# A two-layer non-local block: key products in other banks, theta and transposes at other places, reciprocals a batch sooner

## The chip, the cores and the metric

The kernel runs on one core of one Trainium2 chip. The metric is the device time of one execution in microseconds. Before the change five runs gave 2532.21 to 2532.64 us, with a median of 2532.59 us. One more execution was recorded by the hardware profiler. The engines are named as the profile names them: PE multiplies matrices, PEld loads its weights, DVE is the vector engine, ACT the scalar engine, SP issues DMAs (SPq is its queue).

## The reference

Two layers of the same block are applied to `x` of shape (4, 128, 96, 96) in float32. One layer computes, with `CI` = 64:

```python
g_x     = maxpool2(conv1x1(x, g_w, g_b)).reshape(b, CI, -1).transpose(0, 2, 1)   # values, 2304 keys
theta_x = conv1x1(x, theta_w, theta_b).reshape(b, CI, -1).transpose(0, 2, 1)      # 9216 queries
phi_x   = maxpool2(conv1x1(x, phi_w, phi_b)).reshape(b, CI, -1)                   # keys
f    = einsum('bqc,bck->bqk', theta_x, phi_x)
attn = softmax(f, axis=-1)
y    = einsum('bqk,bkc->bqc', attn, g_x).transpose(0, 2, 1).reshape(b, CI, H, W)
W_y  = conv1x1(y, W_w, W_b)
inv  = bn_gamma * rsqrt(bn_var + 1e-5)
return W_y * inv + (bn_beta - bn_mean * inv) + x
```

## The kernel before, in words

The work is eight blocks (four images by two layers, in the order `ORDER`). A block has nine pairs of query tiles; a pair is 1024 queries (`PT`, two tiles of `QT` = 512). The 2304 keys of a block are 18 tiles of 128 (`NKT`), and two key tiles make a batch (`KB`), so that a pair takes nine batches (`NB`).

The main loop runs over `t`, one batch of one pair for each `t`. In a batch PE makes the scores of two key tiles (`scores`, four products for each tile), ACT takes the exponential of each tile (128x1024, `exp`), DVE adds it to a running sum (`add_up`), and PE multiplies the exponentials of the batch before by the transposed values `gT` (`values`, result `av`). Two pairs make a cycle of 18 batches (`CYCLE`). In it `q` is the number of the cycle's first pair and `s` the batch within the cycle. All else is laid into the cycle at fixed places: the products for new keys (`chunks`) and for new queries (`thetas`) in two halves, one in a batch and one in the next; denominators, reciprocals and the projection with `W` of the pairs that have ended. The order on every engine is that of the code; nothing is rescheduled.

PSUM is cut into three pools: `ps_sc` with two tiles of two banks (scores), `ps_av` with one tile of two banks, and `ps_misc` with two tiles of one bank. Each pool hands out its tiles in turn, so a new tile waits for the readers of the one before the last.

Ahead of the loop the first twelve key tiles of block 0 are made (`FIRST` = 6 batches). A key tile is one group of two products with all 128 input rows (`pooled`, result `gphi_ps`, one bank) and one DVE reduction over 2x2 pixels (`pool`, L226). `batch` then has ACT subtract the mean of the first two key tiles (`centred`, L270) and copy the result to the other half of the partitions (`copied`, L276). In the same stretch come the transposes of the weights (`make_gphi`, `make_theta`, `first_cols`), two square roots with a change of ACT's table, and at its end the queries of the first pair (`theta`, `take_theta`). `square(i, k)` has DVE transpose the values of six key tiles into `gT`, two instructions for each `k`; four of the twelve quarter transposes of block 0 stand ahead of the loop, and the others stand in the loop at the batches that `squares` lists.

In the last cycle (`q == late`) the reciprocals of the pair before the last (`inverses`) stand one in each of four batches, then `normalise` and, at `t == total - 1`, `multiply` and `add`. `ends` holds some `values` products back to that point. The last pair's own denominators follow (`last_denominators`, L374 and L382), then the held products, and the output (`finish`).

Of the kernel before, what the change touches and what calls it, by code (L numbers as in the profile page):

```python
# [9 lines left out]
F32 = mybir.dt.float32  # L10
# [6 lines left out]
P = 128  # L17
B, C, CI, H, W = 4, 128, 64, 96, 96
HW = H * W
NK = (H // 2) * (W // 2)  # L20
QT = 512
# [11 lines left out]
PT = 2 * QT  # L33
NP = HW // PT
KB = 2
# [3 lines left out]
THETAS, SUMS, PROJECT = 5, 2, (8, 12)  # L39
# [9 lines left out]
def shifted_blocks(ctx: ExitStack, tc: tile.TileContext, x: bass.AP, layers, out: bass.AP, flag):  # L49
# [27 lines left out]
    ps_sc = ctx.enter_context(tc.tile_pool(name="ps_sc", bufs=2, space=PSUM))  # L77
    ps_av = ctx.enter_context(tc.tile_pool(name="ps_av", bufs=1, space=PSUM))
    ps_misc = ctx.enter_context(tc.tile_pool(name="ps_misc", bufs=2, space=PSUM))
# [28 lines left out]
    def transposed(src, rows, cols, name, twice=False, ps=None):  # L108
        if ps is None:
            ps = ps_misc.tile([P, QT], F32, tag="misc", name=f"{name}_ps")  # L110
        nc.tensor.transpose(ps[:cols, :rows], src, ident[:rows, :rows])
        t = const.tile([2 * cols if twice else cols, rows], F32, name=name)
        nc.vector.tensor_copy(t[:cols, :], ps[:cols, :rows])
        if twice:
            nc.vector.tensor_copy(t[cols:, :], ps[:cols, :rows])
        return t

    class Layer:
# [22 lines left out]
        def make_gphi(self):  # L141
            self.gphi = transposed(self.gphi_nat, 2 * CI, C, f"gphiT_{self.l}")

        def make_theta(self):
            self.theta = transposed(self.theta_nat, CI, C, f"thetaT_{self.l}")

        def make_scale(self):

# [41 lines left out]
    def two_banks(name):  # L190
        return [ps_misc.tile([P, QT], F32, tag="misc", name=f"{name}_{i}") for i in range(2)]
# [12 lines left out]
    class Block:  # L204
# [25 lines left out]
                ALU.max,  # L230
            )

        def pooled(self, k):

            ps = ps_misc.tile([P, QT], F32, tag="misc", name=f"gphi_ps_{self.name}_{k}")
            for c in range(2):
                nc.tensor.matmul(
                    ps[ts(c, CI), :], lhsT=self.w.gphi[:, ts(c, CI)],
                    rhs=self.chunk(k, slice(0, P)), start=True, stop=True,
                )  # L240
            self.pool(k, ps)

        def chunks(self, j):

# [233 lines left out]
    def denominators(both, folded):  # L478

        pss = two_banks(f"den_ps_{both[0].name}")  # L480

        def make():
            for h in range(2):
                for i in range(len(both)):
                    nc.tensor.matmul(  # L485
                        pss[i][ts(h, CI), :], lhsT=ones[ts(i, CI), :],
                        rhs=folded[ts(i, CI), ts(h, QT)], start=True, stop=True,
                    )

        def take():  # L490
            for pair, ps in zip(both, pss):
                pair.take_denominators(ps, pair.halves[:, QT:])

        return make, take

    def thetas(both):
        pss = two_banks(f"theta_ps_{both[0].name}")

        def part(i, rows, c):
            pair = both[i]  # L500
            return (
                pss[i][ts(c, CI), :], pair.blk.w.theta[rows, :],
                pair.blk.xt[rows, ts(2 * pair.p + c, QT)],
            )

        def take():
            for i in range(2):
                both[i].take_theta(pss[i])

        return crosswise(part, take)  # L510

    ws = [Layer(l, p) for l, p in enumerate(layers)]
# [21 lines left out]
    def begin(n):  # L534

        blocks[n].xt = xs[ORDER[n][0]]
        blocks[n].begin_keys()

    pairs = [Pair(blk, p, n * NP + p) for n, blk in enumerate(blocks) for p in range(NP)]
    total = len(pairs) * NB  # L540
# [10 lines left out]
    b0 = blocks[0]  # L551
# [1 line left out]
    ws[0].make_gphi()  # L553
    busy(WARM[1])
    b0.pooled(0)
    ws[0].make_theta()
    first_cols(ps_sc.tile([P, PT], F32, tag="sc", name="cols_first_ps")[:, :QT])
    b0.pooled(1)
    b0.centring(KB)
    b0.batch(0)  # L560
    for j in range(1, FIRST):
        for k in range(j * KB, (j + 1) * KB):
            b0.pooled(k)
        b0.batch(j)
        if j == 1:
            for w in ws:
                w.make_std()
            nc.scalar.preload_act_table(AF.Exp)
    th = ps_sc.tile([P, PT], F32, tag="sc", name="theta_ps_0")[:, :QT]
    pairs[0].theta(th)  # L570
    pairs[0].take_theta(th)
    for k in range(KT // 32):
        b0.square(0, k)
    xs[1] = load_x(1)
# [5 lines left out]
    }  # L580

    keys = {2 * j: (0, FIRST + j) for j in range(NB - FIRST)}
    squares = {k: [(1, k)] for k in range(4)} | {k: [(2, 2 * k - 10), (2, 2 * k - 9)] for k in (5, 6)}
    spreads, centres = {}, {}
    for n in range(1, len(blocks)):
        cycle = (n - 1) * NP * NB // CYCLE * CYCLE
        for j in range(NB):
            t = cycle + KEYS[j % len(KEYS)] + j // len(KEYS) * CYCLE
# [13 lines left out]
    for t in range(total + 1):  # L602
        q, s = 2 * (t // CYCLE), t % CYCLE
        even, odd = pairs[q : q + 2] if t < total else (None, None)
        first, second, take = None, *pending
        pending = (None, None)
        if t in keys:
            n, i = keys[t]
            if n and i == 0:
                begin(n)  # L610
            first, *pending = blocks[n].chunks(i)
        elif t < total and s == (THETAS if q else THETAS + 2):
            if q < late:
                first, *pending = thetas(pairs[q + 1 : q + 3])
            else:
                first, take = odd.theta_alone()
        elif gone and s == SUMS:
            second, take = denominators(gone, folded)
        elif q == late and s == 11:
            second, take = denominators([even], folded)  # L620
        elif t == total - 1:
            second, take = even.multiply, even.add
        elif gone and s in PROJECT:
            pair = gone[PROJECT.index(s)]
            second, take = pair.multiply, pair.add
        if t < total:
            now, j = divmod(t, NB)
            if s == 0 and q:
                pairs[q - 1].move(folded)
                gone = pairs[q - 2 : q]  # L630
            if s == NB:
                folded = work.tile([P, PT], F32, tag="folded", name=f"folded_{q}", bufs=1)
                even.move(folded)
            if t in loads:
                xs[loads[t]] = load_x(loads[t])
        for i in range(KB):
            if t < total:
                pairs[now].scores(j * KB + i)
            if i == 0 and first:
                first()  # L640
        if second:
            second()
        if gone and s == 1:
            gone[1].fold(folded)
        if q == late and s == 10:
            even.fold(folded)
        for i in range(KB):
            if t < total:
                pairs[now].add_up(j * KB + i)
            if i == 0 and take:  # L650
                take()
        if t - 1 in keys and t < NB:
            b0.batch(keys[t - 1][1])
        if t == total - 1:
            even.note(even.rc)
        if gone and s in (PROJECT[0] - 1, PROJECT[1] - 1):
            pair = gone[s // (PROJECT[1] - 1)]
            pair.note(pair.rc)
        if t:
            before, j = divmod(t - 1, NB)  # L660
            for k in ends.get(t, range(j * KB, (j + 1) * KB)):
                pairs[before].values(k)
        if t < total:
            for i, pair in enumerate(gone):
                if s == 1:
                    pair.add_halves()
                k = s - PROJECT[i] + 5
                if k in range(QT // P):
                    pair.inverses(pair.rc, (k,))
                if k == QT // P - 1:  # L670
                    pair.normalise()
            if s == 13 and q < late:
                even.fold(folded)
            if q == late:
                if s == 10:
                    even.add_halves()
                if s - 13 in range(QT // P):
                    even.inverses(even.rc, (s - 13,))
                if s == 16:
                    even.normalise()  # L680
        if t == total - 1:
            odd.last_denominators()
        if t in centres:
            centres[t].centring(KB)
        for i, k in squares.get(t, []):
            b0.square(i, k)
        for k in range(KT // 32):
            if t - k in spreads:
                blk, i = spreads[t - k]
                if k == 0:  # L690
                    blk.centred(ts(i, GT * KT))
                if k == 1:
                    blk.copied(ts(i, GT * KT))
                blk.square(i, k)
        for step in after.pop(t, []):
            step()
# [324 lines left out]
```

## Time and profile before

| what | value |
|---|---|
| median of 5 runs | 2532.59 us (2532.21 to 2532.64) |
| the profiled execution | 2532.26 us, of it 2530.2 us span from the first to the last instruction |
| granted PE clock | 1.00 |
| PE busy | 2516.2 us (99%) |
| DVE busy | 2167.7 us (86%) |
| ACT busy | 1626.9 us (64%) |
| first exponential of the loop starts | 21.87 us |
| last key reduction ahead of the loop starts | 18.28 us |
| last held `values` products start | 2517.07 us |

The rows of the timeline give the start, the duration, the engine, the line and operation, output and inputs with their shapes, the number of instructions merged into the row, and in brackets how long the engine had been idle and what released it. A merged row's duration reaches to the end of its last instruction. One 32-bit matrix product appears as two MATMUL instructions.

### The profile page before, as it was taken

How to read it: one execution, taken by the hardware profiler on the slowest of the kernel's cores; microseconds unless marked ns; L12 is line 12 of the kernel's file. 1: busy time of each engine (PE TensorE's matmuls, PEld its weight loads, DVE VectorE, ACT ScalarE, POOL GpSimd, SP SyncE). 2: the span in 40 equal slices, each digit the busy share in tenths (PEclk: the TensorE clock that was granted, in tenths of full speed). 3: DMA queues.
4: the chain of work that ended last, by engine and by line, in shares of the span. 5: the costliest groups of instructions: out<-in, count | busy, mean ns of one | idle time of the engine just before them, and what ended most of it. 6: DMA issues, size and time to landing. Idle time of an engine off the chain costs nothing.

```text
span 2530.2 us, 53451 instructions
## 1 busy us (share of the span) xinstructions
PE 2516.2 (99%) x23342; PEld 906.8 (36%) x23342; DVE 2167.7 (86%) x2259; ACT 1626.9 (64%) x1795; POOL 0.7 (0%) x6
## 2 busy tenths in 40 slices
PE   9999999999999999999999999999999999999998
PEld 4333333333333333333333333333333333333333
DVE  6888888888888888888888888888888888888888
ACT  5666666666666666666666666666666666666665
POOL 0000000000000000000000000000000000000000
PEclk9999999999999999999999999999999999999999
DMA  4020000000000000020000000000000000000001
GB/s 159 6 84 9 10 9 6 10 9 10 9 18 14 26 26 26 18 80 10 10 10 18 22 18 26 26 18 10 6 10 10 26 18 15 25 26 26 26 26 39
DMA packets 16661, 60.12 MB, mean 24 GB/s; under 512 B 2650, under 2 KB 3556, under 8 KB 16420
## 3 DMA queue, kind: packets, MB, share of 16 engines
q1 hardware_dynamic: 16252, 56.57, 7.3%
q8 instruction: 184, 3.01, 0.5%
q14 instruction: 57, 0.47, 0.1%
q10 hardware_dynamic: 168, 0.07, 0.0%
HBM read 19.14 MB, written 18.87 MB: 15 GB/s over the span
## 4 chain that ended last, share of the span: by engine, by line


## 5 line engine op out<-in xcount | busy, mean ns | idle before, releaser
L340 ACT ACTIVATE exp<-sc,nshift 128x1024 f32<-128x1024 f32 x1296 | 1386.1, 1113 | 817.4 <-PE sc L334 817.3
L349 DVE TENSOR_TENSOR sum<-sum,exp 128x1024 f32<-128x1024 f32 x1151 | 1408.3, 1224 | 258.5 <-ACT exp L340 209.6
L334 PE MATMUL sc<-theta,phi 64*64 64x512 f32 x10368 | 1252.3, 589 | 2.0 <-ACT theta L328 1.6
L357 PE MATMUL av<-exp,gT 64*64 64x512 f32 x10368 | 1234.7, 589 | 0.2 <-DVE gT L287 0.2
L357 PEld LDWEIGHTS av<-exp,gT 64*64 64x64 f32 x10368 | 399.5, 133 | 714.8 <-issue 690.1
L334 PEld LDWEIGHTS sc<-theta,phi 64*64 64x64 f32 x10368 | 398.9, 133 | 714.7 <-issue 650.3
L400 DVE RECIPROCAL halves<-halves 128x128 f32<-128x128 f32 x284 | 268.6, 946 | 0.0
L200 PE MATMUL gphi_ps<-x,gphiT 64*64 64x512 f32 x1056 | 137.3, 589 | 0.0
L347 DVE TENSOR_TENSOR sum<-exp,exp 128x1024 f32<-128x1024 f32 x72 | 88.2, 1225 | 52.7 <-ACT exp L340 52.0
L226 DVE TENSOR_REDUCE gphi<-gphi_ps 128x128 f32<-128x512 f32 x144 | 92.9, 684 | 30.1 <-PE gphi_ps L200 24.7
L364 ACT COPY halves<-av 128x1024 f32<-128x1024 f32 x71 | 71.9, 1012 | 49.8 <-PE av L357 49.8
L439 DVE SCALAR_TENSOR_TENSOR x<-W_ps,shift,x 128x512 f32<-128x512 f32 x142 | 99.6, 743 | 0.1
L413 DVE TENSOR_TENSOR folded<-folded,sum 64x1024 f32<-64x1024 f32 x71 | 86.3, 1216 | 1.3 <-DMA folded<-sum 0.2
L430 PE MATMUL W_ps<-halves,WT 64*64 64x512 f32 x568 | 74.3, 590 | 2.7 <-DVE halves L424 2.7
L200 PE MATMUL theta_ps<-x,thetaT 64*64 64x512 f32 x560 | 73.6, 589 | 0.0
L287 DVE STREAM_TRANSPOSE gT<-gphi 32x192 f32<-32x192 f32 x192 | 70.6, 368 | 3.5
L200 PEld LDWEIGHTS gphi_ps<-x,gphiT 64*64 64x64 f32 x1056 | 45.1, 132 | 68.3 <-issue 61.2
L424 DVE TENSOR_TENSOR halves<-halves 128x512 f32<-128x512 f32 x71 | 49.1, 692 | 2.4
L421 DVE TENSOR_TENSOR halves<-halves 128x512 f32<-128x512 f32 x71 | 45.7, 685 | 0.0
L417 ACT ACTIVATE halves<-halves 128x512 f32<-128x512 f32 x71 | 44.6, 628 | 1.6 <-DVE halves L424 1.6
L404 ACT ACTIVATE halves<-den_ps 128x512 f32<-128x512 f32 x71 | 41.8, 602 | 1.6 <-DVE halves L421 1.5
L485 PE MATMUL den_ps<-folded,ones 64*64 64x512 f32 x284 | 37.4, 589 | 0.0
(78 smaller groups left out, 235.5 us busy)
## 6 DMA issues: line engine op xcount, KB each, us to landing
folded<-sum SPq DMA_DIRECT2D x71, 256.0 KB
out_dram<-x SPq DMA_DIRECT2D x35, 512.0 KB
x<-in_x_dram SPq DMA_DIRECT2D x18, 768.0 KB
x<-in_x_dram SPq DMA_DIRECT2D x12, 384.0 KB
out_dram<-x SPq DMA_DIRECT2D x4, 128.0 KB
gphi_nat<-in_L_conv_phi_w_dram SPq DMA_DIRECT2D x2, 32.0 KB
rows_other<-in_L_conv_g_b_dram SPq DMA_DIRECT2D x4, 0.2 KB
W_nat<-in_L_conv_W_w_dram SPq DMA_DIRECT2D x2, 32.0 KB
```

Of the source, the lines that this page charges most:

```text
L200: nc.tensor.matmul(out, lhsT=lhsT, rhs=rhs, start=step == 0, stop=step == 1)
L226: nc.vector.tensor_reduce(self.gphi[:, ts(k, KT)].rearrange("p (h w) -> p h w", w=w), ps.rearrange("p (h a w b) -> p h w a b", a=2, b=2, w=w),
L334: nc.tensor.matmul(ps[ts(c, CI), ts(h, QT)], lhsT=self.blk.phi[ts(h, CI), ts(2 * k + c, CI)], rhs=self.th[ts(h, CI), :], start=True, stop= ...
L340: nc.scalar.activation(e, ps, AF.Exp, bias=nshift)
L347: nc.vector.tensor_add(self.sum, self.es[0], e)
L349: nc.vector.tensor_add(self.sum, self.sum, e)
L357: nc.tensor.matmul(self.av[ts(h, CI), ts(r, QT)], lhsT=self.blk.gT[ts(r, CI), k, :], rhs=e[ts(r, CI), ts(h, QT)], start=(k == 0), stop=(k ...
L364: nc.scalar.copy(self.halves, self.av)
L400: nc.vector.reciprocal(self.rc[:, ts(i, P)], src[:, ts(i, P)])
L413: nc.vector.tensor_add(folded[here, :], folded[here, :], self.sum[here, :])
L430: nc.tensor.matmul(self.pss[h][ts(c, CI), :], lhsT=self.blk.w.W[ts(h, CI), ts(c, CI)], rhs=self.y[ts(h, CI), :], start=True, stop=True,)
L439: nc.vector.scalar_tensor_tensor(dst, self.pss[h], self.blk.w.shift, dst, op0=ALU.add, op1=ALU.add)
```

## The change

It has four parts.

1. Ahead of the loop `pooled` makes a batch of two key tiles instead of one tile: both tiles' products, then both reductions. Even batches use the two banks of `ps_misc`, odd batches one two-bank tile of `ps_sc`. The tile of the transposed theta weight moves from `ps_misc` to `ps_sc`, and its transpose comes behind both key tiles of the first batch instead of between them.
2. The queries of the first pair (`theta`, `take_theta`) come behind the products of the fourth batch, ahead of that batch's `centred` and `copied`, instead of behind all six batches.
3. In the first cycle the last four quarter transposes stand all at `t` = 5 instead of two at `t` = 5 and two at `t` = 6, and the two halves of the next queries' products begin at `s` = 6 instead of 7.
4. In the last cycle the four reciprocals and the normalisation of the pair before the last stand one batch sooner: `s` = 12 to 15 instead of 13 to 16.

```diff
-        def make_theta(self):
-            self.theta = transposed(self.theta_nat, CI, C, f"thetaT_{self.l}")
+        def make_theta(self, ps=None):
+            self.theta = transposed(self.theta_nat, CI, C, f"thetaT_{self.l}", ps=ps)
...
-        def pooled(self, k):
-
-            ps = ps_misc.tile([P, QT], F32, tag="misc", name=f"gphi_ps_{self.name}_{k}")
+        def products(self, k, ps):
+
             for c in range(2):
                 nc.tensor.matmul(
                     ps[ts(c, CI), :], lhsT=self.w.gphi[:, ts(c, CI)],
                     rhs=self.chunk(k, slice(0, P)), start=True, stop=True,
                 )
-            self.pool(k, ps)
+
+        def pooled(self, j):
+
+            if j % 2:
+                ps = ps_sc.tile([P, PT], F32, tag="sc", name=f"gphi_ps_{self.name}_{j}")
+                pss = [ps[:, ts(i, QT)] for i in range(2)]
+            else:
+                pss = two_banks(f"gphi_ps_{self.name}_{j}")
+            for step in (self.products, self.pool):
+                for i in range(2):
+                    step(j * KB + i, pss[i])
...
     b0.pooled(0)
-    ws[0].make_theta()
+    ws[0].make_theta(ps_sc.tile([P, PT], F32, tag="sc", name="thetaT_ps")[:, :QT])
     first_cols(ps_sc.tile([P, PT], F32, tag="sc", name="cols_first_ps")[:, :QT])
-    b0.pooled(1)
     b0.centring(KB)
     b0.batch(0)
     for j in range(1, FIRST):
-        for k in range(j * KB, (j + 1) * KB):
-            b0.pooled(k)
+        b0.pooled(j)
+        if j == 3:
+            th = ps_sc.tile([P, PT], F32, tag="sc", name="theta_ps_0")[:, :QT]
+            pairs[0].theta(th)
+            pairs[0].take_theta(th)
         b0.batch(j)
         if j == 1:
             for w in ws:
                 w.make_std()
             nc.scalar.preload_act_table(AF.Exp)
-    th = ps_sc.tile([P, PT], F32, tag="sc", name="theta_ps_0")[:, :QT]
-    pairs[0].theta(th)
-    pairs[0].take_theta(th)
...
-    squares = {k: [(1, k)] for k in range(4)} | {k: [(2, 2 * k - 10), (2, 2 * k - 9)] for k in (5, 6)}
+    squares = {k: [(1, k)] for k in range(4)} | {5: [(2, k) for k in range(4)]}
...
-        elif t < total and s == (THETAS if q else THETAS + 2):
+        elif t < total and s == (THETAS if q else THETAS + 1):
...
-                if s - 13 in range(QT // P):
-                    even.inverses(even.rc, (s - 13,))
-                if s == 16:
+                if s - 12 in range(QT // P):
+                    even.inverses(even.rc, (s - 12,))
+                if s == 15:
                     even.normalise()
```

## Prediction

> **What bounds the kernel now.** I read the page first, for the bound; then the timeline of the first 75 us, of 45 to 62 us and of the last 75 us, since the change touches only these; then the list of waits for the first 25 us.
>
> The page:
>
> ```profile
> PE 2516.2 (99%) x23342; PEld 906.8 (36%) x23342; DVE 2167.7 (86%) x2259; ACT 1626.9 (64%) x1795; POOL 0.7 (0%) x6
> PEclk9999999999999999999999999999999999999999
> ```
>
> PE has work all the time at full clock. The change takes no product away, so it can only win where PE stands still or is held below its pace. A key group, a score tile, a `values` tile or half of a key or query step each take PE 0.86 us (the score tiles' rows follow each other by that). From the score tile at 24.75 to the `values` row at 51.41 I count 31 such units: 26.6 us for 26.66. So PE has no gap there, and what is saved ahead is kept. The same holds for the 2,400 us behind. Three gaps are left. The first is ahead of the loop:
>
> ```profile
> PEld gphi_ps L237 <- DVE gphi L226: 6.8, 9, 1.2
> PEld sc L334 <- ACT theta L328: 2.5, 1, 2.5
> ...
> 18.28 0.69 DVE L226 TENSOR_REDUCE gphi<-gphi_ps 128x128 f32<-128x512 f32 x1 [0.17 <-PE gphi_ps L237]
> 19.54 0.40 ACT L276 COPY phi<-phi 64x256 f32<-64x256 f32 x1
> 19.97 0.69 ACT L328 ACTIVATE theta<-theta_ps,cols_first 128x512 f32<-128x512 f32 x1
> 20.71 1.09 PE L334 MATMUL sc<-theta,phi 64*64 64x512 f32 x8 [1.62 <-ACT theta L328]
> 21.87 1.11 ACT L340 ACTIVATE exp<-sc,nshift 128x1024 f32<-128x1024 f32 x1 [1.21 <-PE sc L334]
> 24.75 1.09 PE L334 MATMUL sc<-theta,phi 64*64 64x512 f32 x8 [0.38 <-ACT exp L340]
> ```
>
> Groups wait for a bank (two take 1.87 us, 14.42 to 16.29, where PE needs 1.72), and the loop starts only after the chain last reduction, `centred`, `copied`, theta, scores, exponential. PE runs freely from the fourth score tile (24.75). The second gap is in the first cycle, the third in the last:
>
> ```profile
> 51.02 1.52 DVE L287 STREAM_TRANSPOSE gT<-gphi 32x192 f32<-32x192 f32 x4
> 52.59 0.21 PEld L357 LDWEIGHTS av<-exp,gT 64*64 64x64 f32 x8 [1.04 <-DVE gT L287]
> ...
> 2510.73 0.95 DVE L400 RECIPROCAL halves<-halves 128x128 f32<-128x128 f32 x1
> 2511.71 0.69 DVE L424 TENSOR_TENSOR halves<-halves 128x512 f32<-128x512 f32 x1
> 2512.32 1.22 DVE L349 TENSOR_TENSOR sum<-sum,exp 128x1024 f32<-128x1024 f32 x1
> 2512.45 1.09 PE L430 MATMUL W_ps<-halves,WT 64*64 64x512 f32 x8 [2.68 <-DVE halves L424]
> 2515.18 0.20 PEld L374 LDWEIGHTS den_last_ps<-sum,ones 128*64 128x64 f32 x4 [0.81 <-DVE x L439]
> ```
>
> PE waits for transposed values, and at the end for the normalisation.
>
> **Part 1 and 2, ahead of the loop.** Nothing is added or removed: 24 key products, 12 reductions, 6 times `centred` and `copied`, one theta. The rows give the sizes: reductions start 0.61 apart in a row; the first starts 1.1 us after its group's start; ACT's copy starts 0.53 after its `centred`, the next work 0.43 later. The loads of x are SP's and are not moved; SP waits for each to land before it issues the load eight further on, so its rows show landings: the fourth by 10.29, then one about every 0.95 (11.44, 12.39, 13.32, 14.30).
>
> - Group 0 starts at 5.29 as before, group 1 straight behind it at 6.48 (was 7.45). Its reduction: 7.56. DVE's copy of the theta weight now stands behind it: 8.17 to 8.39. Group 2 takes that copy's tile, so PE idles until 8.44 (before: group 2 by 8.36).
> - Groups 2 and 3: 8.44 to 10.21 (1.72, and 0.05 that a start from a stop costs). In the changed order the two reductions of an odd batch share one wait, for all four products: 10.43 and 11.04, end 11.73. Batch 1 on ACT at 11.77 (was 11.25), 0.5 late. Behind it are queued two roots and the table load, so batch 2 starts at 14.52 (was 14.00), theta at 15.47, batch 3 at 16.1. What covers this 0.5: the next thing ACT must wait for, reductions 9 (ends 17.28) and 11.
> - PE from here without a bank to wait for: groups 4 and 5 at 10.32 (the fourth load) to 12.09, 6 and 7 to 13.80, theta to 14.66, 8 and 9 to 16.38, 10 and 11 to 18.10. The loads land ahead of each.
> - Reductions 10 and 11: 18.31 and 18.92, end 19.62. `centred` 19.64, `copied` 20.17, first exponential 20.60 (was 21.87: the theta of 0.69 and the score tile behind it have left the chain, but the last reduction comes 0.64 later).
> - PE meanwhile: first scores 18.10, half a key step, second scores 19.82 (their tile is free at 19.62). Third scores wait for the first exponential to end: 21.77. The fourth wait for the second, which now follows without a gap (20.60 + 1.01 + 1.12 = 22.73): 22.77, was 24.75. **Saved: 1.98 us.** The transposes (eight by 0.38 from 19.63) end at 22.7, ahead of the sum and of `values` at 24.5.
>
> [...] Group 0's pass starts, 5.29 and 6.05, are 0.76 apart, later ones 0.43. [...] I take the row, and keep 1.1 as the lower end. Upper end: were the odd reductions not to share a wait, 2.6.
>
> **Part 3.** Four transposes of 0.38 move ahead of the two sums of `t` = 6. They then end at about 49.95 on the clock of before, and `values` needs them at 51.41: the wait goes. It cost 52.59 less the 51.84 at which that instruction was due: **0.75 us** saved. The sums move back by 1.5 us and catch up in two batches; who waits for them is an exponential seven tiles on, which is 6 us away. The query products keep their 2 x 0.86 us. ACT's two takings of 0.69 then stand ahead of exponentials 16 and 17 instead of behind; scores 16 are due at 55.0 and the takings end at 54.25, so they cost nothing; uncovered they would cost up to 0.6. Bounds 0.5 to 0.8.
>
> **Part 4.** DVE is busy without a gap from 2494.5 to 2515, so the part only changes what stands first. Pitches from its rows: sum to sum 1.33, sum to reciprocal 1.14, reciprocal to sum 0.86, to normalisation 0.98, and 0.61 on to a sum. Starting from the sum at 2496.96: reciprocals at 2498.10, 2501.43, 2504.76, 2508.10, normalisation 2509.08, and the last sum 2512.35, about where it was. Each exponential is there before its sum. So `W_ps` runs at 2509.83 (was 2512.45), and the two `values` tiles behind it end at 2512.5. What is late next is the last sum: it ends at 2513.56, and the denominators start at 2513.6 instead of 2515.19. DVE's `add` (2 x 0.67) ends at 2514.9, as the first denominator comes (2514.73). What follows on PE is the same chain: **1.58 us** saved. The output DMA that `add` issues on SP stays at about 2515, and those of `finish` come behind it as before. Lower end 1.1 (a sum or reciprocal held half a microsecond), upper 1.7.
>
> **Sum.** 1.98 + 0.75 + 1.58 = 4.31 us. The profiled execution, 2532.26 (span 2530.2), would be 2527.95. It lies 0.33 under the median of the runs, so the median goes from 2532.59 to 2528.3, which is 0.17%.
>
> **The rivals.** A difference of 0.2%, about what a measurement of this kernel can tell from no change, is 5.07 us: faster begins below 2527.5, slower above 2537.7.
>
> - *The start wins nothing, since the first scores wait for batch 5.* If their wait covered the whole key tile, they would start at 20.6, the first exponential at 21.75, the fourth scores at about 24.6. With 0.15 + 0.75 + 1.58 the time is 2530.1. Against it: in the trace scores 4 start at 28.24, ahead of the key batch at 29.10 that stands before them in the code. Chance 0.10.
> - *All terms at their upper ends*: 2.6 + 0.8 + 1.7 = 5.1, time 2527.5 or less. Against it: the shared wait. Chance 0.17 that it passes the bound.
> - *Slower: PE falls back to half clock in the new idle stretch.* PE has only two small transposes between 7.34 and 8.44. If the clock fell there and stayed low for the ten groups and theta (11 x 0.86 = 9.46 us), these take 9.46 more; less 4.31 that is 5.15 slower, 2537.7. It decides from 8.6 us of slow running. Against it: full pace follows directly on idle stretches of 1.62 us (20.71) and 2.68 us (2512.45). For it: the slow passes at 5.29. Chance 0.06, with any wait that recurs in each cycle.
> - That the change is not made as told is excluded by its instruction order: the moves are there, and no product is added.
>
> **How the numbers follow.** The forecast, 2528.3, has 0.67. Its own range is 2527.5 (5.1 saved) to 2529.9 (1.1 + 0.5 + 1.1 = 2.7 saved). The first rival reaches to 2530.1; with the ends of its terms I take 2527.1 to 2530.6 for 8 in 10. Faster 0.17; same 0.67 + 0.10 = 0.77; slower 0.06.
>
> **What would show it.** In the changed trace: group 2 at 8.4; odd reductions in pairs; the first exponential at 20.6 and the fourth score tile at 22.8; no wait of `values` for `gT` near 50 us; `W_ps` at about 2507.1 and the denominators at about 2510.9 (each 2.73 earlier than above), with PE idle between. Wrong would be: a fourth score tile later than 24, slow passes behind 6.5, or denominators that still follow `values` without a gap.

## The result and the profile after

The changed kernel takes 2527.36 us (median of 21 runs, 2526.84 to 2528.18), the kernel before 2532.64 us (median of 41 runs beside them, 2531.93 to 2534.64). The ratio is 0.9978, with a 95% interval of 0.9972 to 0.9984. The difference of the medians is 5.28 us. The forecast was 2528.3 us and 4.31 us saved, with "same" as the likeliest case (0.77). The kernel became faster: the interval lies clear of no change, at 4.1 to 7.1 us saved. The measured saving is a little above the bound of 5.07 us that the prediction set for "faster", and the interval reaches to both sides of that bound.

The page of the changed kernel, engines and instructions:

```profile
PE 2514.7 (100%) x23342; PEld 909.4 (36%) x23342; DVE 2167.2 (86%) x2259; ACT 1625.8 (64%) x1795; POOL 0.7 (0%) x6
```

The instruction counts are those of before. PE's share has risen to 100%: time in which it stood still is gone. The timeline of the start (start, duration, engine, line, output and inputs, idle time ahead):

```profile
18.42 1.09 PE L343 MATMUL sc<-theta,phi 64*64 64x512 f32 x8
...
18.53 1.29 DVE L226 TENSOR_REDUCE gphi<-gphi_ps 128x128 f32<-128x512 f32 x2 [1.02 <-PE gphi_ps L236]
...
19.86 0.50 ACT L279 ACTIVATE phi<-gphi,centre 64x256 f32<-64x256 f32 x1 [1.38 <-DVE gphi L226]
...
20.39 0.40 ACT L285 COPY phi<-phi 64x256 f32<-64x256 f32 x1
...
20.82 2.12 ACT L349 ACTIVATE exp<-sc,nshift 128x1024 f32<-128x1024 f32 x2
...
21.99 2.09 PE L343 MATMUL sc<-theta,phi 64*64 64x512 f32 x16 [0.76 <-ACT exp L349]
```

The steps are those forecast, each some 0.2 us later: the last two reductions come as a pair behind both products, theta has left the chain, the first scores no longer wait, and the first exponential starts at 20.82 instead of 21.87. The 0.2 us come in at group 4, which starts at 10.55 where 10.32 was forecast. In a second trace of the changed kernel it starts at 10.34, and the first exponential at 20.57 (forecast 20.60). In the first cycle the wait for transposed values is gone:

```profile
45.14 3.05 DVE L296 STREAM_TRANSPOSE gT<-gphi 32x192 f32<-32x192 f32 x8
...
48.22 5.21 DVE L358 TENSOR_TENSOR sum<-sum,exp 128x1024 f32<-128x1024 f32 x4
...
50.51 1.97 PE L366 MATMUL av<-exp,gT 64*64 64x512 f32 x16
```

The eight transposes run in one piece, the four sums catch up behind them, and the `values` row has no idle time in brackets and is not broken into a pair and a rest. The last cycle:

```profile
2505.98 0.69 DVE L433 TENSOR_TENSOR halves<-halves 128x512 f32<-128x512 f32 x1
...
2506.59 3.88 DVE L358 TENSOR_TENSOR sum<-sum,exp 128x1024 f32<-128x1024 f32 x3
2506.72 1.09 PE L439 MATMUL W_ps<-halves,WT 64*64 64x512 f32 x8
2507.63 1.90 PE L366 MATMUL av<-exp,gT 64*64 64x512 f32 x16
...
2510.51 0.65 PE L383 MATMUL den_last_ps<-sum,ones 128*64 128x256 f32 x4 [0.98 <-DVE sum L358]
...
2512.39 3.66 PE L366 MATMUL av<-exp,gT 64*64 64x512 f32 x32
```

`W_ps` follows the scores without the 2.68 us of idle time that it had, and the denominators wait about 1 us for DVE's last sum, as foretold.

One table holds what is read from all the traces below. "Full rate from" is the first entry of the trace's record of PE's clock. Ahead of it the rows show half pace: with 8 filling products, where full rate comes at 7.49, the four instructions of the first key group (5.32 to 7.29) take 1.97 us, and the four of theta, later on, 1.03. A later start of exponential 3 means a later start of all behind it; "3", "9", "18" count the loop's exponentials from 0. The fourth column is the first cycle with its wait, the last is the end.

| kernel | full rate from | exp 3 starts | exp 9 to exp 18 | last exp to denominators |
|---|---|---|---|---|
| before | 5.89 | 25.91 | 20.04 | 5.18 |
| changed | 6.12 | 24.15 | 18.89 | 3.42 |
| changed, again | 6.19 | 23.91 | 18.89 | 3.40 |
| parts 1 and 2 | 4.54 | 23.56 | 20.05 | 6.76 |
| part 3 | 6.06 | 25.98 | 18.88 | 6.88 |
| part 4 | 4.45 | 25.60 | 20.04 | 3.41 |
| part 2 alone | 6.74 | 24.48 | 20.04 | 6.75 |
| transposes alone | 6.68 | 26.29 | 18.88 | 6.89 |
| queries alone | 5.22 | 25.88 | 19.18 | 5.18 |
| 8 filling products | 7.49 | 26.54 | 20.04 | 5.19 |
| 18 filling products | 7.47 | 26.51 | 20.04 | 7.11 |
| longer idle stretch | 6.36 | 23.99 | 18.88 | 5.47 |
| other banks | 5.59 | 22.94 | 18.89 | 3.42 |
| other banks, denominators in other order | 5.93 | 23.41 | 18.88 | 2.36 |

Between exponential 18 and the last one all of these take the same time within 0.02 us.

### The profile page after: what moved, and what is told of

Its sections match the earlier page's. It is cut to its first block, busy times and chain, and to the rows that moved or that the text cites. A ratio compares the mean times of both kernels' runs of the same rounds, so it can differ in the third digit from the quotient of the medians.

```text
span 2526.0 us, 53450 instructions
## 1 busy us (share of the span) xinstructions
PE 2514.7 (100%) x23342; PEld 909.4 (36%) x23342; DVE 2167.2 (86%) x2259; ACT 1625.8 (64%) x1795; POOL 0.7 (0%) x6
## 4 chain that ended last, share of the span: by engine, by line
```

## Experiments: each part alone

**Parts 1 and 2 alone.** The changed kernel with the edits to `squares`, `THETAS` and `inverses` taken back.

> The kernel before with parts 1 and 2 alone (key products in pairs of banks, theta behind the fourth batch). By the prediction's sum the fourth score tile of the loop comes 1.98 us sooner and the run takes 2530.6 us. By the trace of the changed kernel (exponentials 3 to 12 start 1.75 us sooner) it is 1.75 us: 2530.8. A rival: the start wins less alone, because the wait for transposed values at t = 6 stands at the same batch and grows when all ahead of it comes sooner; then exponential 18 would start less than 1.75 us sooner, and the time be above 2531.2.

Measured: 2531.44 us (11 runs) against 2532.97 (32 runs of the kernel before on that chip), ratio 0.9992, 0.9983 to 1.0001. So the runs alone decide nothing; their median lies above 2531.2, where the rival had put it. The trace decides, if rows with nearly the same start of the clock are compared: against part 4 alone (4.45 and 4.54), whose start is the old one, exponential 3 comes 25.60 - 23.56 = 2.04 us sooner; the pair at 6.06 and 6.12 (part 3 alone, changed) gives 25.98 - 24.15 = 1.83, and with the second trace of the changed kernel (6.19, 23.91) it is 2.07. The rival falls: the first cycle takes 20.05 as before. But the last column was a surprise: 6.76 instead of 5.18, at an end that nothing had touched.

**Part 3 alone.** The kernel before with

```diff
-    squares = {k: [(1, k)] for k in range(4)} | {k: [(2, 2 * k - 10), (2, 2 * k - 9)] for k in (5, 6)}
+    squares = {k: [(1, k)] for k in range(4)} | {5: [(2, k) for k in range(4)]}
-        elif t < total and s == (THETAS if q else THETAS + 2):
+        elif t < total and s == (THETAS if q else THETAS + 1):
```

> The kernel before with part 3 alone (all last transposes at t = 5, query products one batch sooner in the first cycle). The prediction says 0.75 us saved: 2531.8 us. The theory from the two traces: one half of the rows of PE runs on by one product while the other half waits, and stays behind until the loop's next even point, so the wait costs 0.75 + 0.43 = 1.18 us: 2531.4 us, and exponential 18 starts 1.1 to 1.2 us sooner. A rival: what goes beyond 0.75 comes from the start (parts 1 and 2) and not from here; then exponential 18 starts 0.75 us sooner.

Measured: 2533.12 us (11 runs, 2530.72 to 2533.78), ratio 0.9996, 0.9987 to 1.0005. By the runs it wins nothing. By the trace exponential 18 follows exponential 9 by 18.88 instead of 20.04 us, 1.16 saved, and this is lost again behind the last exponential, where the denominators come 6.88 instead of 5.18 us later. The trace of this kernel shows where; first its timeline, then windows of PE (the window, its length, PE busy, instructions in brackets, granted clock, and last the share and rate of DMA):

```profile
2511.37 1.97 PE L430 MATMUL W_ps<-halves,WT 64*64 64x512 f32 x8 [2.68 <-DVE halves L424]
2513.09 2.78 PE L357 MATMUL av<-exp,gT 64*64 64x512 f32 x16
2515.80 0.65 PE L374 MATMUL den_last_ps<-sum,ones 128*64 128x256 f32 x4
```

```profile
2508.00:2510.00 2.00, 0.69 (x8) 1.00 0.00 0
2510.00:2512.00 2.00, 0.63 (x4) 0.86 0.00 0
2512.00:2514.00 2.00, 2.00 (x16) 0.50 0.04 8
2514.00:2516.00 2.00, 2.00 (x18) 0.79 0.20 80
2516.00:2518.00 2.00, 2.00 (x20) 1.00 0.45 182
```

Behind the idle stretch of 2.68 us PE is granted half its clock: `W_ps` takes 1.97 instead of 1.09 us, `values` 2.78 instead of 1.90. In the profiled execution of the kernel before, the `values` row and the windows, which read 1.00 throughout, are:

```profile
2513.36 1.90 PE L357 MATMUL av<-exp,gT 64*64 64x512 f32 x16
```

```profile
2510.00:2512.00 2.00, 0.00 (x0) 1.00 0.00 0
2512.00:2514.00 2.00, 1.55 (x16) 1.00 0.03 8
2514.00:2516.00 2.00, 2.00 (x20) 1.00 0.08 31
```

So the old end has two lengths. Four of the six traces of kernels that have it whole and unfilled show the longer one (6.75 to 6.89 us against 5.18), which costs 1.57 to 1.71 us. Each of the six traces comes with the time of its own execution. With the gain that its part has ahead of the end added back (1.16 and 0.86 in the first cycle, 2.04 and 1.81 at the start), the four with the longer end come to 2533.50, 2534.46, 2534.47 and 2534.63 us, the two with the shorter to 2532.04 and 2532.26. The runs of the kernel before lie in two groups at the same places, with only 3 of 121 between 2533.2 and 2533.5 us.

**Part 4 alone.** The kernel before with `s - 12` and `s == 15` in place of `s - 13` and `s == 16`.

> The kernel before with part 4 alone (reciprocals and normalisation of the pair before the last one batch sooner). The prediction says 1.58 us saved: 2531.0 us. By the trace of the changed kernel the denominators of the last pair start 1.76 us sooner: 2530.8. A rival: DVE is busy there without a gap, and the order of its work alone wins nothing, so that the denominators come as late as before: 2532.6. Another: the tail behind the last product also gets shorter when the first outputs leave sooner; then the runs show over 2 us, below 2530.6.

Measured: 2530.55 us (11 runs, 2530.00 to 2531.51), ratio 0.9989, 0.9980 to 0.9998. The end takes 3.41 instead of 5.18 us, so 1.77 is saved and the first rival falls. The runs gain 2.4 us in the median, as the second rival had it, but not in the tail: that is 7.10 us in this trace and 6.69 before. The clock accounts for it: with this part the idle stretch of 2.68 us is gone, and with it the executions in which half clock follows (in its trace the windows from 2500 to 2520 us read 1.00). Of the 32 runs beside it 15 lie above 2533.4; at 1.57 to 1.71 us each that is 0.8 us in the mean, with the 1.77 about 2.5, and the means differ by 2.65. The 11 runs lie within 1.5 us, those of the kernel before within 3.4.

**The whole once more**, beside the three parts on one chip.

> The changed kernel once more, on the same chip as the three parts alone. If the parts are independent, the savings of the three together are its own: 1.75 + 1.16 + 1.76 = 4.67 us by the trace (4.31 by the prediction), against the 5.28 us by which the medians of the first runs differ. If the 0.6 us between is in the tail behind the last product, a second profile shows a tail shorter than the 7.15 us of the first; if it is noise between runs, the difference here is nearer to 4.7 us.

Measured: 2527.53 us (10 runs), ratio 0.9976, 0.9967 to 0.9986. The tail, from the start of the last product to the end, is 6.80 us in this trace, 7.14 in the first one and 6.69 before, and in the other kernels from 6.50 to 7.68: it varies by itself and is no gain. The parts add up: 1.83 to 2.04 ahead, 1.15 in the first cycle, 1.76 at the end, together 4.74 to 4.95 us with PE at full clock. The medians here differ by 5.44 us.

## Experiments: the clock behind an idle stretch

If half clock in part of the executions makes the kernel before slower, then filling the stretch must take these executions away, and lengthening the stretch that the changed kernel still has must bring them back.

**Filling, first try.** Between scores and `multiply` of the last batch:

```diff
+        if t == total - 1:
+            fill = ps_sc.tile([P, PT], F32, tag="sc", name="fill_ps")
+            for i in range(FILL):
+                nc.tensor.matmul(fill[:, :P], lhsT=ident, rhs=ident, start=True, stop=True)
```

> The kernel before with 18 products of 128x128 that nothing reads, put on PE behind the last scores, where it stands still 2.7 us ahead of W_ps. Nothing of the computation is changed. Theory: in some executions of the kernel before the granted clock of PE is 0.50 right behind this idle stretch (so in the traces of the kernels with the first part alone and with the cycle part alone, where W_ps and the values products take 0.85 us for each pair instead of 0.43) and the end is 1.6 to 1.7 us longer; with the stretch filled this goes, no run lies in an upper group above 2533.4 us, the median is 2532.2 to 2532.6 and the clock stays 1.00. Rival: the upper group comes from elsewhere (the start, loads); then a third of the runs stays above 2533.4 us. Second rival: the filling products delay W_ps; then the denominators start over 5.2 us behind the last exponential at full clock.

Measured: 2534.84 us (11 runs, 2533.92 to 2535.87). The second rival held: 18 products are 36 passes and took 4.29 us, so `W_ps` came 1.9 us late. The clock stayed at 1.00, but the times can't be compared. The profiled execution took 2535.86 us at full clock: its start is late (exponential 3 at 26.51) and its tail long (7.68), so a run can be long for these reasons too.

**Filling, with 8 products.**

> The kernel before with 8 products of 128x128 that nothing reads (16 passes by 0.117 us as in the run with 18, so 1.9 us) on PE behind the last scores; nothing of the computation is changed. Theory: W_ps is not delayed now, the 2.7 us stretch is cut into two pieces under 0.8 us, so the granted clock stays 1.00 to the end in every execution: all runs between 2531.8 and 2533.2 us, where 40% of the runs of the kernel before lie above 2533.4. Rival: the upper group has another cause; then a third or more of the runs stays above 2533.4 us.

```profile
2510.80 2.05 PE L645 MATMUL fill_ps<-ident 128*128 128x128 f32 x16 [0.39 <-ACT exp L340]
2513.09 1.09 PE L430 MATMUL W_ps<-halves,WT 64*64 64x512 f32 x8 [0.24 <-DVE halves L424]
```

Measured: 2532.76 us (11 runs); ten lie from 2531.74 to 2533.35, one at 2535.84. Against the 18 runs beside it the ratio is 0.9998, 0.9989 to 1.0007, so the middle of the runs does not move; it is the upper group that counts. `W_ps` is not delayed (5.19 to the denominators). Of the 121 runs of the kernel before taken in all, 48 lie above 2533.4 us, their median 1.9 us above that of the other 73 (2534.27 and 2532.39). Were the share of 40% still there, one or none of 11 would come in 3 of 100 series; with the 6 of 18 seen beside it, in 7 or 8. So PE with more to do very likely loses the upper group. The single run at 2535.84 has no trace and stays open.

**A longer stretch in the changed kernel.**

```diff
+        if t == total - 1:
+            idle = work.tile([P, 384], F32, tag="idle", name="idle", bufs=1)
+            for i in range(4):
+                nc.vector.tensor_add(idle, odd.es[14][:, :384], odd.es[14][:, 384:768])
```

> The changed kernel with four more sums of 128x384 on DVE ahead of the last batch's sums (their result is not used). Theory 1: at the changed end DVE is the bound, and 4 x 0.45 = 1.8 us on it move the denominators of the last pair and the end by 1.8 us: 2529.2 us. Rival to it: PE is the bound, and up to 1.1 us of it is hidden: 2528.1. Theory 2: the idle stretch of PE ahead of the denominators grows from 1.1 to 2.9 us, and the half clock comes back in part of the runs, which are then up to 1.7 us longer (up to 2531). Rival to it: the stretch stands elsewhere in time and no run is longer than 2529.8.

```profile
2512.40 1.12 PE L383 MATMUL den_last_ps<-sum,ones 128*64 128x256 f32 x4 [3.04 <-DVE sum L358]
2513.31 1.06 PE L383 MATMUL den_last_ps<-exp,ones 128*64 128x256 f32 x4
```

```profile
2510.00:2512.00 2.00, 0.00 (x0) 0.93 0.00 0
2512.00:2514.00 2.00, 1.60 (x8) 0.50 0.00 0
2514.00:2516.00 2.00, 2.00 (x14) 0.71 0.65 262
```

Measured: 2531.94 us (11 runs). Three lie from 2529.56 to 2529.96, eight from 2531.66 to 2532.94; the profiled one is of the eight. Theory 1 holds: all of the delay on DVE shows (5.47 - 3.42 = 2.05 us to the denominators, so DVE is the bound there), and the three shorter runs lie where this puts them. Theory 2 holds in kind: with 3.04 us of idle time the half clock is back, and the products of the denominators take 1.12 and 1.06 instead of 0.65 and 0.60 us. It does not hold in size. The eight longer runs are 2.3 us above the three, and above the 2531 set as the highest; in the trace half clock makes the way from the denominators to the held `values` products only 1.33 us longer (3.21 instead of 1.88). What adds the rest is open.

**When it falls.** In each of the five traces with half clock at the end (parts 1 and 2, part 3, part 2 alone, transposes alone, longer stretch) the record shows it for 3.413 us, from 2505.383 us after the start of full rate on, though the kernels and the idle stretches differ. In part 3 alone that is at 2511.44, 0.07 us behind the idle stretch (2508.69 to 2511.37). In the kernel before the stretch is as long (2509.77 to 2512.45), full rate came at 5.89, and the clock stayed at 1.00. Why one stretch of 2.68 us is followed by half clock and another is not, no run shows. How often it happens is estimated from the runs alone: their upper group, 48 of 121, is 40%. Around the stretch of about 1 us that the change leaves, the windows of both traces of the changed kernel and of that of part 4 alone read 1.00.

The start of the loop moves with the start of full rate. The seven kernels with the old start show exponential 3 at 25.60, 25.88, 25.91, 25.98, 26.29 and 26.51 to 26.54 as full rate comes at 4.45, 5.22, 5.89, 6.06, 6.68 and 7.47 to 7.49. This alone moves a run by up to 0.9 us.

## Experiments: what in parts 1 to 3 does it, and more of the same

**Part 2 alone:** theta behind the fourth batch, the key products as before.

> The kernel before with part 2 alone: the first queries behind the fourth batch, the key products one tile at a time in two banks as before. Theory: the theta taking (0.69 us) and the score products behind it leave the chain, while PE's added 0.86 us is hidden in its waits for a bank; the last reduction comes about 0.3 us later (18.6), ACT's last copy ends at 20.3, the first exponential starts at 20.3 to 20.6 and the fourth score tile at 22.6, so the saving is about the 1.75 to 1.98 us of parts 1 and 2 together, and part 1 by itself gives nothing. Rival: part 1 is needed, since groups wait for a bank at 0.94 us each; then the last reduction comes 0.8 us later and the saving is 1.2 us or less.

Measured: 2532.34 us (11 runs, 2530.88 to 2533.10), ratio 0.9995, 0.9986 to 1.0004; its old end was at half clock in the trace. Exponential 3 starts at 24.48 with full rate from 6.74, and with the old start at 26.29 (6.68): 1.8 us saved. Parts 1 and 2 together save 1.83 to 2.07, so the other banks add 0.3 us at most. The saving is that of the theory, its steps only in part: the last reduction comes 0.7 us later (19.40 against 18.67), as the rival had it, and the first exponential 1.17 us sooner (21.08 against 22.25). The rest is won behind it, where the first four exponentials now follow one another without a gap.

**The transposes alone, the query products alone** (one profiled execution each).

> The kernel before with the last transposes all at t = 5 and the query products left at s = 7. Theory: the transposes alone take the wait away, and with it the lag of one half of the rows: exponential 18 comes 1.1 to 1.2 us sooner than exponential 9 does (so it was with both edits). Rival: the query products must move too, since they stand ahead of other work; then 0.8 us or less.

> The kernel before with the query products of the first cycle at s = 6 and the transposes left where they are. Theory: half of a query step (0.86 us) stands ahead of the waiting values, so that the wait of 0.75 us goes by being filled, and as the products are only moved nearly the whole 1.1 us is won as well; the transposes are then needed for nothing. Rival: the values products stand ahead of the query products on PE, the wait stays, and exponential 18 against exponential 9 is as before (0.0 to 0.2 us).

From exponential 9 to 18: 18.88 us with the transposes alone, the full gain of 1.16 us, so that their theory holds. With the query products alone it is 19.18 us, 0.86 gained: less than the theory's 1.1, and far more than the rival's 0.2. The two don't add; both together give 18.89. The rows of PE there, first transposes alone, then queries alone, where the row of the weight load (PEld) shows the wait:

```profile
51.79 1.97 PE L357 MATMUL av<-exp,gT 64*64 64x512 f32 x16
53.51 1.97 PE L334 MATMUL sc<-theta,phi 64*64 64x512 f32 x16
```

```profile
51.39 1.11 PE L200 MATMUL theta_ps<-x,thetaT 64*64 64x512 f32 x8
52.24 2.27 PE L357 MATMUL av<-exp,gT 64*64 64x512 f32 x16
...
52.57 0.24 PEld L357 LDWEIGHTS av<-exp,gT 64*64 64x64 f32 x7 [0.19 <-DVE gT L287]
...
53.96 2.26 PE L334 MATMUL sc<-theta,phi 64*64 64x512 f32 x16
55.68 0.59 PE L357 MATMUL av<-exp,gT 64*64 64x512 f32 x1
```

Four of these products run side by side: eight instructions take 1.11 us, hardly more than two that follow each other (1.02 in the row at 51.41 below). With the query products in front, one product of `values` starts at 52.24; the three beside it still wait for transposed values until 52.57. So `values` takes 2.27 instead of 1.97 us, and a single instruction splits off behind it. These 0.3 us are what is missing.

**Other banks for the first batches.** The last pair of reductions waits for both products (18.53 above). With the batches' banks exchanged each of the last two waits for its own:

```diff
-            if j % 2:
+            if j % 2 == 0:
-    first_cols(ps_sc.tile([P, PT], F32, tag="sc", name="cols_first_ps")[:, :QT])
+    first_cols()
```

> The changed kernel with the banks of the first batches exchanged: even batches in one two-bank tile of the score pool, odd ones in two small banks, and the three columns transposed in a small bank. Theory: the last batch's first reduction then waits for its own two products alone and starts 0.7 us sooner, the second 0.2 us sooner, so the first exponential and all behind it come 0.4 to 0.6 us sooner: 2526.8 us. Rival: the reductions are not what is late, or the first batch's pair, which now shares one wait, delays group 2 by as much; then 2527.3 us or more.

```profile
16.08 2.48 DVE L226 TENSOR_REDUCE gphi<-gphi_ps 128x128 f32<-128x512 f32 x4 [1.81 <-PE gphi_ps L236]
...
19.56 2.17 ACT L349 ACTIVATE exp<-sc,nshift 128x1024 f32<-128x1024 f32 x2
```

Measured: 2526.41 us (8 runs, 2526.21 to 2527.15), ratio to the kernel before 0.9973, 0.9962 to 0.9983. The last four reductions follow one another without a gap and end at 18.56 instead of 19.82; the first exponential starts 1.26 us sooner. By the medians 0.95 to 1.1 us is won over the changed kernel (2527.36 and 2527.53), twice what was expected; the two kernels did not run side by side. The expectation counted only the last reductions; the trace shows that PE is ahead before that, with group 2 at 7.64 instead of 8.54 (it takes a bank that is free) and the products of theta at 13.29 instead of 14.00.

**The same, and the last exponential's products first in the denominators:**

```diff
-                for part in (self.sum, self.es[NKT - 1]):
...
+            for part in (self.es[NKT - 1], self.sum):
+                for i in range(2):
```

> The changed kernel with the other banks for the first batches (which gave 1.0 us), and in the last pair's denominators the products of the last exponential ahead of those of the sum, for both tiles. Theory: PE stands still 1.1 us ahead of them because DVE's last sum ends so late; two of the four groups (0.86 us) now run in that stretch, the held values follow 0.86 us sooner, and the run takes 2525.5 us. Rival: behind that the four reciprocals on DVE (3.4 us) decide the end, not PE, and it gains 0.4 us: 2526.0.

```profile
2508.72 1.08 PE L386 MATMUL den_last_ps<-exp,ones 128*64 128x256 f32 x8
...
2509.78 1.08 PE L386 MATMUL den_last_ps<-sum,ones 128*64 128x256 f32 x8
...
2510.79 3.66 PE L366 MATMUL av<-exp,gT 64*64 64x512 f32 x32
```

The held `values` products start 2510.79 - 2506.36 = 4.43 us behind the start of the last exponential instead of 2512.39 - 2507.09 = 5.30: the 0.86 us expected. The last product, too, ends 0.86 us sooner against the last exponential (11.05 us behind it, 11.91 with the other banks alone), so the reciprocals of the rival do not hold PE up. The runs show little of it: 2526.28 us in the median, seven of eight from 2525.81 to 2526.78, ratio 0.9973, 0.9962 to 0.9984. One took 8291 us, which nothing here explains. The tail behind the last product grew from 6.67 to 7.10 us between the two traces. Whether it took the gain or the few runs hide it is open; both versions beat the changed kernel by about 1 us.

## Why the prediction was wrong, and where it was right

- **Parts 1 and 2, 1.98 us: right.** 1.83 to 2.07 at nearly equal starts of the clock. Each step came as written, group 2 at 8.54 for 8.44 and the fourth scores at about 23.0 for 22.8. Moving theta does nearly all of it. The lower end of 1.1 is a term that no run shows. Full rate came at 4.45 to 7.49 over the traces and in no kernel with part 1 later than 6.36, and what parts 1 and 2 saved was never below 1.83 us.
- **Part 3, 0.75 us: mechanism right, size wrong.** The failed step is "It cost 52.59 less the 51.84 at which that instruction was due". Measured: 1.15. The rows of the kernel before:

```profile
51.41 1.02 PE L357 MATMUL av<-exp,gT 64*64 64x512 f32 x2
...
53.52 0.59 PE L334 MATMUL sc<-theta,phi 64*64 64x512 f32 x1
53.93 0.60 PE L357 MATMUL av<-exp,gT 64*64 64x512 f32 x3
```

  Two instructions in 1.02 us are one product alone. Of the four that run side by side, one went on at 51.41 and three waited until 52.59; behind them the rows still show one in front and three behind (53.52 and 53.93). A score tile is whole only with its last products, so what counts are the three, and they were due at 51.41 with the first: 52.59 - 51.41 = 1.18 us. The two kernels with this wait changed agree: without it 1.16 us comes back, and with 0.3 us of it left, 0.86.
- **Part 4, 1.58 us: size too small.** 1.76 at full clock. The failed step is the pitch "sum to sum 1.33": the pairs of sums between the reciprocals take 2.49 us in the changed kernel, so that one follows the other by 1.27 us; three times 0.06 is the 0.18.

```profile
2502.58 2.49 DVE L358 TENSOR_TENSOR sum<-sum,exp 128x1024 f32<-128x1024 f32 x2
```

- **The term at nothing: half clock at the old end.** The prediction priced half clock only as a danger in the new idle stretch, and wrote against it: "full pace follows directly on idle stretches of 1.62 us (20.71) and 2.68 us (2512.45)". That was one execution. By the two groups of runs, half clock follows the second stretch in about 40% of them (48 of 121), and part 4 takes it away. With 1.57 to 1.71 us each this is 0.65 us in the mean: 4.85 + 0.65 = 5.5, and the means of all runs differ by 5.70 (2533.15 of 121, 2527.45 of 31). The five runs known ahead lay within 0.43 us, all in the lower group. With a share of 40% that happens in 8 of 100 series: bad luck, but the stretch of 2.68 us and the danger of half clock both stood in the prediction.
- **The forecast of "same".** The step "A difference of 0.2%, about what a measurement of this kernel can tell from no change" failed first: the measured interval reaches 0.06%, or 1.5 us, to each side, so that even the 4.31 us of the sum would have stood clear of no change. To pass the 5.07 us it took both: the two sizes alone give 4.85, half clock alone 4.31 + 0.65 = 4.96. In the medians half clock counts for less. The lower group of all runs of the kernel before lies 4.89 us above the changed kernel (2532.39 of 73, 2527.50 of 31), that of the 41 runs in the result alone 5.08 (2532.44, 2527.36). So which side of 5.07 the median falls on is within the noise; that the kernel is faster is not.
- **The rivals.** The start won (against the first). The terms at their upper ends (5.1) came near in size, but for another reason than the reductions. The slower rival had the right mechanism in the wrong kernel: at the start of the changed one PE idles 0.58 us ahead of group 2, and full pace stayed (its windows from 8 to 20 us read 1.00). Its "8.6 us of slow running" is where the saving of 4.31 us would be used up; for 5.07 us slower it would take 18.8. The measured time lies within the 8 in 10 range, 2527.1 to 2530.6, and beyond the own range of the sum, 2527.5.

## What to carry to other kernels

One profiled execution shows one of several ways that an execution can go. Here half clock followed the idle stretch of 2.68 us in four of six traces and, by the groups of the runs, in about 40% of the executions. The one trace and the five runs without it, known ahead, did not show that it stays away: it was a cost that the change removed. When products run side by side and some of them wait, the wait is counted from the time at which those that wait were due, with the first of their group (here 1.18 us, not 0.75). And of two moves against one wait, one can be enough (1.16 us with the transposes alone, 1.15 with both).

## What was unexpected of the hardware

In four of six traces the granted clock was halved for 3.413 us behind an idle stretch of 2.68 us, at a cost of 1.57 to 1.71 us; in the other two it was not. Of four products of 64x64 side by side, one ran ahead of the three others by a whole product and stayed ahead, so that its scores started at 53.52, before the last `values` instructions of the others at 53.93. A filling product of 128x128 in float32 takes two passes of about 0.11 us (36 passes take 4.29 us, 16 take 2.05); with eight of them, doing nothing, ten of eleven runs stayed out of the longer group.
